# Attention with keys in the partitions of the scores, and one written-out order for TensorE

## The chip, the cores and the metric

The kernel runs on one core of a Trainium2 chip. The metric is the device time of one execution in microseconds (us). The core has five engines that run their own instruction streams: TensorE (PE; its weight loads are listed as PEld), VectorE (DVE), ScalarE (ACT), GpSimd (POOL) and SyncE (SP), which here issues all DMA transfers.

## The reference

One transformer block on 2048 tokens of width 1024, in float32: layernorm, causal attention with 16 heads of 64 and rotary embedding, layernorm, residual; then a gated feed-forward part with 4-bit weights (looked up from codes and scaled), again with layernorms and a residual.

```python
q = rotary((hidden @ Wq).reshape(b, s, 16, 64)); k = rotary(...Wk); v = ...Wv
logits = einsum('bhqd,bhkd->bhqk', q, k)
logits = where(causal, logits, -1e9) / sqrt(64)
attn = softmax(logits, axis=-1)
out = einsum('bhqk,bhkd->bhqd', attn, v).reshape(b, s, 1024) @ Wo
...
x = x + layernorm(attention(layernorm(x)))
x = x + layernorm(ffn(layernorm(x)))      # ffn: (silu(x Wg) * (x Wu)) Wd
```

## The kernel before

Float32 products are made of pieces. Each operand is split into a high part in the fp32r type (a ScalarE copy) and the rest (a VectorE subtraction); `split` does both. A product is then the sum of high x high, high x low and low x high, three passes on TensorE (`mm3`, lines 114 to 116).

The kernel has four stages. The ramp normalizes and transposes the input and makes q, k and v of the first two pairs of heads. The attention stage makes the q, k and v of the other six pairs (24 groups of `qkv`, one for each pair m and each 512 tokens c) beside the attention of the pairs that are ready. Then the output projection (`project`), the residual and the second transposition follow, and at last the feed-forward part, which the change does not touch.

Attention works on blocks: one head h and 512 queries (index J), 64 blocks in all. In a block the scores have the queries in the partitions: for each of its four 128-query tiles j and each 512 keys i, two products (lines 255 and 257: the high part of q against the stacked high and low parts of k, then the low part of q) and, on the diagonal, a third that adds the causal mask (line 259). Over a block's life:

- VectorE takes the row maximum of each 128x512 piece (line 261), ScalarE the exponential with that maximum as its bias, and sums it along the row at the same time (line 262).
- Small VectorE operations (lines 267 to 279) make one factor for each piece of a row, from the maxima and sums, with a reciprocal of two elements per partition; GpSimd multiplies the probabilities by it (line 284).
- For the product with v the keys must be in the partitions, so TensorE transposes each 128x128 piece of the probabilities (line 294, 2176 in all), `split` takes the two parts from the transposed bank, and two products with v (lines 298 and 299) add them up in the bank `o`. v holds its high part in columns 0 to 63 and its low part in 64 to 127, so the two halves of `o` are added at the end (lines 301 and 302).

There are eight PSUM banks: one for the q/k/v products and the projection ("F"), three for scores ("S"), three for transposes ("T"), one for `o` ("O").

The order of instructions on each engine is made by a scheduler, which lets the instruction streams run in a simulated time and takes what is ready, in the order of the program. Some q/k/v products are tied to a score product by a hand-made dependency (`after`, used in `pace`, with PACE = 0.85), so that they are spread over the attention beside them. All transfers go through SP's one queue. q, k and v pass through DRAM: `load_q` and `load_kv` bring a block's q and a head's k and v back in.

Of the kernel before, what the change touches and what calls it, by code (L numbers as in the profile page):

```python
# [22 lines left out]
D = 64  # L23
# [7 lines left out]
PACE = 0.85  # L31
# [3 lines left out]
BATCH = 2  # L35
STEP = 4
FIRST = (0, 1, 2, 3)
ORDER = (0, 3, 1, 2)
# [19 lines left out]
def block_kernel(ctx, tc, x, wq, wk, wv, wo, gu_codes, gu_scales, d_codes, d_scales, cos_sin, out):  # L58
# [12 lines left out]
    BANKS = {"F": 1, "S": 3, "T": 3, "O": 1}  # L71
    BANK_ORDER = ("F", "S", "S", "S", "T", "T", "T", "O")
# [8 lines left out]
    turn = [0]  # L81
# [5 lines left out]
    ident = const.tile([P, P], F32, name="ident")  # L87
    make_identity(nc, ident)
    ident_b = const.tile([P, P], BF, name="ident_b")
    V.tensor_copy(ident_b, ident)  # L90
    mask_f = slot("t2", [P, P], F32, "mask_f")
    G.memset(mask_f, 0.0)

    G.affine_select(out=mask_f, in_=mask_f, compare_op=ALU.is_ge, fill=MASK, base=0, pattern=[[-1, P]], channel_multiplier=1)
    mask_b = const.tile([P, P], BF, name="mask_b")
    V.tensor_copy(mask_b, mask_f)
# [6 lines left out]

    def f32(ap):
        return ap.bitcast(F32)
# [37 lines left out]
    def transposed(row, tiles, cs):  # L143

        for g in range(0, KE, 4):
            pt = bank("T", "pt").rearrange("p (k n) -> p k n", k=4)
            for k in range(4):
                T.transpose(pt[:, k], row[:, (g + k) * P : (g + k + 1) * P], ident)  # L148
            for k in range(0, 4, 2):
                d = tiles[(g + k) // 2]  # L150
                split(d[:, 0, :, cs], d[:, 1, :, cs], pt[:, k : k + 2])
# [54 lines left out]
    def qkv(m, c, ws, xs, ramp=False, pace=None):  # L206
# [3 lines left out]
        for n, w in enumerate(ws):  # L210
            o = bank("S" if ramp and n != 1 else "F", "qkv")
            for k in range(KE):
                mm = mm3(o, w[k], xs[k // 2][:, :, k % 2, :], k == 0, k == KE - 1)
                if k == 0 and pace:
                    pace(mm, n)
            t1 = slot("t2", [P, 512], F32, "t1")
            if n == 2:
                A.copy(t1, o)
                pv = bank("F", "pv").rearrange("p (t n) -> p t n", t=4)
                for t in range(4):  # L220
                    T.transpose(pv[:, t, :], t1[:, t * P : (t + 1) * P], ident)
# [5 lines left out]
            else:  # L227
                A.copy(t1, o)
                sh = slot("t2", [P, 512], F32, "sh")
                V.stream_shuffle(sh, t1, [i ^ 1 for i in range(32)])  # L230
                V.tensor_tensor(t1, t1, tab[:, 0, :], ALU.mult)
# [5 lines left out]


    def scores(J, q, k, anchors):

        prob = []
        nh = J + 1
        for j in range(4):
            t = 4 * J + j
            w = (t + 1) * P
            if j % BATCH == 0:
                mxs = small.tile([P, BATCH, 4], F32, tag="mxs", name="mxs")[:, :, :nh]
                sums = small.tile([P, BATCH, 4], F32, tag="sums", name="sums")[:, :, :nh]
            for i in range(nh):
                b, e = i * 512, min(i * 512 + 512, w)  # L250
                if j == 0:
                    prob.append(slot("pa", [P, 4, 512], F32, "prob"))
                diag = e == w
                s = bank("S", "s")[:, : e - b]
                mm = T.matmul(s, lhsT=q[:, 0, j * P : (j + 1) * P], rhs=k[:, b:e], start=True, stop=False)  # L255
                anchors.append(((anchors[-1][0] if anchors else 0) + e - b, mm))
                T.matmul(s, lhsT=q[:, 1, j * P : (j + 1) * P], rhs=k[:, b:e], start=False, stop=not diag)  # L257
                if diag:
                    T.matmul(s[:, e - b - P :], lhsT=ident_b, rhs=mask_b, start=False, stop=True)
                mx = mxs[:, j % BATCH, i : i + 1]  # L260
                V.tensor_reduce(mx, s, AX.X, ALU.max, negate=True)  # L261
                A.activation(prob[i][:, j, : e - b], s, AF.Exp, bias=mx, accum_out=sums[:, j % BATCH, i : i + 1])  # L262
            if j % BATCH < BATCH - 1:
                continue
            rc = small.tile([P, BATCH, 4], F32, tag="rc", name="rc")[:, :, :nh]
            if nh == 1:
                V.reciprocal(rc, sums)
            else:

                nm = small.tile([P, BATCH, 1], F32, tag="nm", name="nm")  # L270
                V.tensor_reduce(nm, mxs, AX.X, ALU.min)
                cf = small.tile([P, BATCH, 4], F32, tag="cf", name="cf")[:, :, :nh]
                V.tensor_tensor(cf, mxs, nm.to_broadcast([P, BATCH, nh]), ALU.subtract)
                A.activation(cf, cf, AF.Exp, scale=-1.0)
                sm = small.tile([P, BATCH, 1], F32, tag="sm", name="sm")
                V.tensor_tensor(sums, sums, cf, ALU.mult)
                V.tensor_reduce(sm, sums, AX.X, ALU.add)
                V.reciprocal(sm, sm)
                V.tensor_tensor(rc, cf, sm.to_broadcast([P, BATCH, nh]), ALU.mult)  # L279
            for i in range(nh):  # L280
                for jj in range(j - BATCH + 1, j + 1):
                    n = min(512, (4 * J + jj + 1) * P - i * 512)
                    p = prob[i][:, jj, :n]
                    G.tensor_scalar(p, p, rc[:, jj % BATCH, i : i + 1], 0.0, ALU.mult, ALU.add)  # L284
        return prob

    def weighted(h, J, prob, v):
        o = bank("O", "o")
        nk = 4 * J + 4
        for kb in range(nk):  # L290
            j0 = max(0, kb - 4 * J)
            pt = bank("T", "pt")
            for j in range(j0, 4):
                T.transpose(pt[:, j * P : (j + 1) * P], prob[kb // 4][:, j, kb % 4 * P : (kb % 4 + 1) * P], ident)  # L294
            cs = slice(j0 * P, 512)
            pw = slot("pw", [P, 2, 512], FR, "pw")
            split(pw[:, 0, cs], pw[:, 1, cs], pt[:, cs])
            T.matmul(o[:, cs], lhsT=v[:, kb, :], rhs=pw[:, 0, cs], start=kb == 0, stop=False)  # L298
            T.matmul(o[:, cs], lhsT=v[:, kb, :], rhs=pw[:, 1, cs], start=False, stop=kb == nk - 1)  # L299
        ol = slot("ol", [D, 512], F32, "ol")  # L300
        A.copy(ol, o[D:P, :])
        V.tensor_tensor(ol, o[:D, :], ol, ALU.add)
        load(at[J][h * D : (h + 1) * D, :], ol)

    def load_kv(h, k, v, cs):

        m, r = h // 2, h % 2 * D
        for a in range(2):
            load(f32(k[a * D : (a + 1) * D, cs]), ks[m][r : r + D, a, cs])
        load(f32(v[:, cs.start // P : cs.stop // P]), vs[m][cs, h % 2, :].rearrange("(t p) n -> p t n", p=P))  # L310

    def load_q(h, q, J):

        m, r = h // 2, h % 2 * D
        for a in range(2):
            load(f32(q[a * D : (a + 1) * D]), qs[m][r : r + D, :, J * 512 : J * 512 + 512])
# [13 lines left out]
    def both(*steps):  # L330
        for m, c in steps:
            qkv(m, c, first[m], xs[c], ramp=True)
# [8 lines left out]
    def new_kv():  # L341
        return slot("hd", [P, S], FR, "k"), slot("hd", [P, NT, P], FR, "v")

    def new_q():

        q = slot("hd", [P, 2, 2, 512], FR, "q")
        return [q[:, 0], q[:, 1]]

    def attend(h, J, q, k, v, anchors):
        weighted(h, J, scores(J, q, k, anchors), v)  # L350

    every = slice(0, S)
    parts = [slice(c * 512, (c + 1) * 512) for c in range(NC)]

    later = [(m, c) for m in range(2, KE) for c in range(NC)][:-2]
    ws = {}

    def group(m, c, xs=None, pace=None):
        if m not in ws:
            ws[m] = prep_qkv(m)  # L360
        qkv(m, c, ws[m], xs or load_x(c), pace=pace)

    for pair in range(KE - 1):
        anchors = []
        now = [later[g] for g in range(len(later)) if g * (KE - 1) // len(later) == pair]
        own = now and now[0][0] == pair
        for h in (2 * pair, 2 * pair + 1):
            k, v = new_kv()
            by_part = h == 0 or (own and h % 2 == 0)
            if not by_part:  # L370
                load_kv(h, k, v, every)
            if h % 2 == 0 and not own:
                if now[0][0] not in ws:
                    ws[now[0][0]] = prep_qkv(now[0][0])
                ready = load_x(now[0][1])
            order = FIRST if by_part else ORDER
            qj = {}
            for i, J in enumerate(order):
                if by_part:
                    if own and J == now[0][1]:  # L380
                        group(*now.pop(0))
                    load_kv(h, k, v, parts[J])
                if i % 2 == 0:
# [351 lines left out]
```

## Time and profile before

| what | value |
|---|---|
| time, median of 3 runs | 3121.71 us (3119.2 to 3123.59) |
| the profiled execution's own time | 3127.5 us |
| its span, first to last instruction | 3125.7 us |
| PE busy | 3003.9 us (96%) |
| DVE busy | 2161.1 us (69%) |
| ACT busy | 1831.5 us (59%) |
| POOL busy | 702.8 us (22%) |
| mean granted TensorE clock | 0.982 of full speed |

The durations in the next part come from the profiled execution, which is one execution; the span is what its engines' instructions cover, and its own time is a little longer. A group's row in the profile reads: line, engine, operation, output <- inputs by the program's names, shapes, number of instructions, then busy time in us and mean ns of one, and last the idle time of the engine just before these instructions and what ended most of it. The spans of matmuls overlap, because TensorE is pipelined: the distance from one start to the next is what a matmul costs, not its span.

### The profile page before, as it was taken

What the parts mean: (1) busy time and instruction counts of PE and PEld (TensorE: products, weight loads), DVE (VectorE), ACT (ScalarE), POOL (GpSimd) and SP (SyncE); (2) the same over time, 40 slices, a digit from 0 to 9 for tenths busy, and PEclk for the clock granted to TensorE, in tenths of its full rate; (3) what the DMA queues carried; (4) which work ended last, traced back from release to release, by engine and by line L of the source; (5) the groups of instructions that cost most, each with busy time, mean ns of one, the idle gap of its engine ahead of it and who ended that gap; (6) DMA issues with size and microseconds to landing.
All of it is one profiled execution on the core that took longest, in us unless ns stands there. A gap on an engine that the chain in (4) does not pass through costs nothing.

```text
span 3125.7 us, 43392 instructions
## 1 busy us (share of the span) xinstructions
PE 3003.9 (96%) x14656; PEld 2470.5 (79%) x14656; DVE 2161.1 (69%) x4428; ACT 1831.5 (59%) x3846; POOL 702.8 (22%) x888
## 2 busy tenths in 40 slices
PE   7979999999998999989988999999999999999998
PEld 6868888787877787778767888888888888888887
DVE  7457778687777777776574987666776669868322
ACT  3246667676766666676554876555665558657211
POOL 5344344343433443454222000000000000000000
PEclk9989999999999999999989999999999999999999
DMA  8777666557547656462355332222322226867785
GB/s 312 250 234 224 209 207 197 178 163 222 181 161 191 200 191 196 165 202 67 113 186 193 122 128 95 93 90 102 103 99 90 93 101 213 278 218 246 254 305 197
DMA packets 246495, 552.31 MB, mean 177 GB/s; under 512 B 20224, under 2 KB 110336, under 8 KB 219136
## 3 DMA queue, kind: packets, MB, share of 16 engines
q1 hardware_dynamic: 246272, 549.53, 53.8%
q8 instruction: 116, 1.90, 0.3%
q14 instruction: 107, 0.88, 0.1%
HBM read 403.70 MB, written 145.75 MB: 176 GB/s over the span
## 4 chain that ended last, share of the span: by engine, by line
PE 42%; DMA 3%; DVE 3%; ACT 1%; issue 1%; SPq 0%; DVEq 0%; POOLq 0%; POOL 0%; ACTq 0%
PE bk L114 13%; PE bk L116 13%; PE bk L115 13%; DMA cs<-in_d_codes 1%; DMA out<-xt 1%; PE pj L440 0%; PE pj L441 0%; PE pj L442 0%; DMA it<-ind 0%; DMA y<-yd 0%; DVE mp L511 0%; DMA cs<-in_d_scales 0%; PE pt L148 0%; DVE st L126 0%; DVE mp L504 0%
## 5 line engine op out<-in xcount | busy, mean ns | idle before, releaser
L498 ACT ACTIVATE ln<-cs,bias 128x512 f32<-128x512 f32 x910 | 611.8, 719 | 136.0 <-DVE mp L504 38.4
L114 PE MATMUL bk<-x,wt 128*128 128x512 f32 x1376 | 535.8, 390 | 0.0
L115 PE MATMUL bk<-x,wt 128*128 128x512 f32 x1376 | 535.4, 389 | 0.0
L116 PE MATMUL bk<-x,wt 128*128 128x512 f32 x1376 | 535.2, 389 | 0.0
L284 POOL TENSOR_SCALAR prob<-prob,rc 128x512 f32<-128x512 f32 (+3 forms) x640 | 408.1, 660 | 408.9 <-DVE rc L279 245.2
L262 ACT ACTIVATE prob<-s,mxs 128x512 f32<-128x512 f32 (+3 forms) x640 | 401.4, 630 | 161.2 <-DVE mxs L261 147.0
L121 DVE TENSOR_TENSOR pw<-pt,pw 128x512 fp32r<-128x512 f32 (+3 forms) x640 | 377.8, 602 | 135.1 <-ACT pw L120 133.4
L261 DVE TENSOR_REDUCE mxs<-s 128x1 f32<-128x512 f32 (+3 forms) x640 | 380.1, 602 | 96.3 <-PE s L257 57.7
L120 ACT CAST pw<-pt 128x512 fp32r<-128x512 f32 (+3 forms) x640 | 323.5, 526 | 165.4 <-PE pt L294 134.7
L132 POOL TENSOR_TENSOR rs<-ve,nhalf 128x1 f32<-128x1 f32 x64 | 40.0, 637 | 1552.2 <-DVE ve L130 1546.3
L294 PE MATMUL pt<-ident,prob 128*128 128x128 f32 x2176 | 347.1, 276 | 5.1 <-DVE pw L121 4.8
L294 PEld LDWEIGHTS pt<-ident,prob 128*128 128x128 f32 x2176 | 267.8, 142 | 59.3 <-issue 7.5
L255 PE MATMUL s<-k,q 128*128 128x512 f32 (+3 forms) x640 | 266.8, 417 | 36.9 <-ACT prob L262 35.4
L115 PEld LDWEIGHTS bk<-x,wt 128*128 128x128 f32 x1376 | 258.6, 188 | 53.9
L114 PEld LDWEIGHTS bk<-x,wt 128*128 128x128 f32 x1376 | 258.7, 188 | 53.5
L116 PEld LDWEIGHTS bk<-x,wt 128*128 128x128 f32 x1376 | 258.4, 188 | 53.7
L114 PE MATMUL bk<-wd,it 128*128 128x512 f32 x672 | 261.6, 389 | 1.2 <-DMA it<-ind 1.2
L115 PE MATMUL bk<-wd,it 128*128 128x512 f32 x672 | 261.4, 389 | 0.0
L116 PE MATMUL bk<-wd,it 128*128 128x512 f32 x672 | 261.3, 389 | 0.0
L299 PE MATMUL o<-pw,v 128*128 128x512 f32 (+3 forms) x640 | 250.6, 394 | 4.9 <-DVE pw L121 4.6
L298 PE MATMUL o<-pw,v 128*128 128x512 f32 (+3 forms) x640 | 247.1, 387 | 6.1 <-ACT pw L120 5.5
L114 PE MATMUL qkv<-xc,w 128*128 128x512 f32 x576 | 235.8, 409 | 13.0 <-ACT w L173 7.4
(124 smaller groups left out, 5514.2 us busy)
## 6 DMA issues: line engine op xcount, KB each, us to landing
xc<-xd SPq DMA_DIRECT2D x96, 1024.0 KB, 8.8
it<-ind SPq DMA_DIRECT2D x84, 1024.0 KB, 7.0
ind<-hl SPq DMA_DIRECT2D x84, 512.0 KB, 2.6
q<-qs SPq DMA_DIRECT2D x128, 256.0 KB, 7.1
cs<-in_gu_scales SPq DMA_DIRECT2D x172, 128.0 KB, 3.1
cs<-in_gu_codes SPq DMA_DIRECT2D x86, 256.0 KB, 2.9
tab<-in_cos_sin SPq DMA_DIRECT2D x32, 512.0 KB, 9.8
xd<-xr SPq DMA_DIRECT2D x16, 1024.0 KB, 6.8
```

What stands on the lines that cost most here:

```text
L114: r = T.matmul(o, lhsT=w[:, 0], rhs=xx[:, 0], start=first, stop=False)
L115: T.matmul(o, lhsT=w[:, 0], rhs=xx[:, 1], start=False, stop=False)
L116: T.matmul(o, lhsT=w[:, 1], rhs=xx[:, 0], start=False, stop=last)
L120: A.copy(hi, src)
L121: V.tensor_tensor(lo, src, f32(hi), ALU.subtract)
L255: mm = T.matmul(s, lhsT=q[:, 0, j * P : (j + 1) * P], rhs=k[:, b:e], start=True, stop=False)
L261: V.tensor_reduce(mx, s, AX.X, ALU.max, negate=True)
L262: A.activation(prob[i][:, j, : e - b], s, AF.Exp, bias=mx, accum_out=sums[:, j % BATCH, i : i + 1])
L284: G.tensor_scalar(p, p, rc[:, jj % BATCH, i : i + 1], 0.0, ALU.mult, ALU.add)
L294: T.transpose(pt[:, j * P : (j + 1) * P], prob[kb // 4][:, j, kb % 4 * P : (kb % 4 + 1) * P], ident)
L299: T.matmul(o[:, cs], lhsT=v[:, kb, :], rhs=pw[:, 1, cs], start=False, stop=kb == nk - 1)
L498: A.activation(ln, c8, AF.Identity, bias=bias_of[ab], scale=ab[0])
```

## The change

The scores are made with the keys in the partitions, so that the exponentials already lie as the product with v needs them. The 2176 transposes of line 294 are gone, and so are the small rescaling operations and GpSimd's scaling. What they did is done in other ways:

- Row maxima: `maxima` makes a separate score pass, queries in the partitions, from the high part of q alone with the stacked k, into the one bank "T"; VectorE reduces it as before. When a block's pieces are done, the minimum of the negated maxima is turned into one row by four small products with the identity and a ScalarE copy (`row`). That row is stored in partition 0 of a second q tile, against which a second k tile (`kb`) has ones, so that the maximum is subtracted inside the score product.
- Probabilities: `probabilities` makes two products per 128 keys (lines 375 and 376), the exponential is written into the same bank, and `split` takes both parts from there.
- Row sums: GpSimd adds the high parts of a block's probabilities (lines 393 and 395). The low parts are summed by TensorE: `vb` holds ones beside the high part of v, so that the second product with v (line 404) gives the sums in its upper 64 partitions, in a bank of its own ("L", two of them). At the block's end the GpSimd sums are split and added with two products against ones (`total`), and a VectorE reciprocal of 64x512 and a GpSimd product scale the output.
- TensorE's order: the work of the attention stage is laid out in steps, one for each 128 keys of a block. In each step come loads (rank 0), a score product (1), a maxima product (2), up to six products of the q/k/v groups or the projection (3, at 3.35 a step in the mean), and the products with v of two steps before (4). `chain` ties every TensorE instruction of this stage to the one before it.
- Banks: "T" has one in place of three, "L" two. Each block issues eight loads (three of k, three of q, two of v), and k and v are loaded block by block for every head.
- The masks and the identity are in fp32r in place of bf16, and the rotary product reads the bank in place of its copy in SBUF.

```diff
-    BANKS = {"F": 1, "S": 3, "T": 3, "O": 1}
+    BANKS = {"F": 1, "S": 3, "T": 1, "O": 1, "L": 2}
...
-                V.tensor_tensor(t1, t1, tab[:, 0, :], ALU.mult)
+                V.tensor_tensor(t1, o, tab[:, 0, :], ALU.mult)
...
+    def load_block(h, J):
...
+        for a in range(2):
+            load(f32(ka[a * D : (a + 1) * D, cs]), ks[m][r : r + D, a, cs])
+        load(f32(kb[D:, cs]), ks[m][r : r + D, 0, cs])
...
+        for a in range(2):
+            load(f32(q[a * D : (a + 1) * D, 0]), qs[m][r : r + D, 0, cs])
+        load(f32(q[D:, 1]), qs[m][r : r + D, 1, cs])
+        ts = slice(4 * J, 4 * J + 4)
+        load(f32(va[:, ts]), vs[m][cs, h % 2, :].rearrange("(t p) n -> p t n", p=P))
+        load(f32(vb[:, ts, :D]), vs[m][cs, h % 2, :D].rearrange("(t p) n -> p t n", p=P))
...
+    def chain(mm):
+        if tail:
+            after(mm, tail[-1])
+        tail[:] = [mm]
+        return mm
...
+    def maxima(h, J, j, i):
...
+        s = bank("T", "mx")[:, : e - b]
+        chain(T.matmul(s, lhsT=q[:, 0, j * P : (j + 1) * P], rhs=ka[:, b:e], start=True, stop=not diag))
+        if diag:
+            chain(T.matmul(s[:, e - b - P :], lhsT=ident_r, rhs=mask_q, start=False, stop=True))
...
+        V.tensor_reduce(mx[:, j, i : i + 1], s, AX.X, ALU.max, negate=True)
...
+            def row():
+                r = bank("T", "row")
+                for jj in range(4):
+                    chain(T.matmul(r[:1, jj * P : (jj + 1) * P], lhsT=nm[:, jj : jj + 1], rhs=ident_r, start=jj == 0, stop=jj == 3))
+                A.copy(q[:1, 1], r[:1])
...
+    def probabilities(u, h, J, kb):
...
+        chain(T.matmul(s[:, cs], lhsT=ka[:, ks_], rhs=q[:, 0, cs], start=True, stop=False))
+        chain(T.matmul(s[:, cs], lhsT=kb_[:, ks_], rhs=q[:, 1, cs], start=False, stop=diag is None))
+        if diag:
+            chain(T.matmul(s[:, diag], lhsT=ident_r, rhs=mask_k, start=False, stop=True))
...
+        A.activation(s[:, cs], s[:, cs], AF.Exp)
...
+        split(pw[:, 0, cs], pw[:, 1, cs], s[:, cs])
...
+        if kb == 0:
+            G.tensor_copy(acc, f32(pw[:, 0]))
+        else:
+            G.tensor_tensor(acc[:, cs], acc[:, cs], f32(pw[:, 0, cs]), ALU.add)
+
+    def weighted(u, h, J, kb):
...
+        chain(T.matmul(o[:, cs], lhsT=va[:, kb], rhs=pw[:, 0, cs], start=kb == 0, stop=end))
+        chain(T.matmul(ls[:, cs], lhsT=vb[:, kb], rhs=pw[:, 1, cs], start=kb == 0, stop=False))
+        if not end:
+            return
+        y = acc[:D, 1]
+        A.copy(y, o[D:, :])
+        V.tensor_tensor(y, o[:D, :], y, ALU.add)
+        a2 = slot("pb", [P, 2, 512], FR, "a2")
+        split(a2[:, 0], a2[:, 1], acc[:, 0])
+
+        def total():
+            chain(T.matmul(ls, lhsT=ones_l, rhs=a2[:, 0], start=False, stop=False))
+            chain(T.matmul(ls, lhsT=ones_l, rhs=a2[:, 1], start=False, stop=True))
+            V.tensor_tensor(y, ls[:D, :], y, ALU.add)
+            r = acc[:D, 0]
+            V.reciprocal(r, ls[D:, :])
+            G.tensor_tensor(y, y, r, ALU.mult)
+            load(at[J][h * D : (h + 1) * D, :], y)
...
+        later.append((4, total))
...
+    fill = rest()
+    for step in range(min(work), max(work) + 8):
...
+        for rank in range(5):
+            if rank == 3 and step >= 0:
+                for _ in range(MOST):
+                    if spent >= PACE * (step + 1):
+                        break
+                    mm = next(fill, GAP)
+                    if mm is GAP:
+                        break
+                    chain(mm)
+                    spent += 1
+            for e in work.get(step, ()):
+                if e[0] == rank:
+                    e[2](*e[3])
```

## The prediction

> **What bounds the kernel now.** I read the windows first, to find where the change can act. The ramp's last first-pass product starts at 173 us and the last product with v ends at 1545 us, so the attention stage is 1372 us of the 3125.7 us span; a window in the feed-forward part stands below it as a yardstick for TensorE at full rate.
>
> ```profile
> 173.00:1545.00 1372.00, 1303.77 (x7106) 1065.97 (x7104) 1005.13 (x2281) 899.16 (x2319) 577.57 (x758) 0.97 0.59 184
> 2000.00:3000.00 1000.00, 999.42 (x4410) 827.28 (x4409) 677.81 (x1176) 571.44 (x904) 0.91 (x2) 1.00 0.46 156
> ```
>
> After the window's length come PE, PEld, DVE, ACT and POOL busy time with counts, then clock, DMA share, GB/s. The lower row gives the price of one 512-wide product: 1000 us / 4410 = 0.227 us. The upper row shows TensorE nearly always occupied, VectorE 73%, ScalarE 66%, GpSimd 42%. The PE timeline then shows what a transpose costs:
>
> ```profile
> 600.62 0.23 PE L298 MATMUL o<-pw,v 128*128 128x128 f32 x1
> 600.69 0.61 PE L294 MATMUL pt<-ident,prob 128*128 128x128 f32 x4
> 601.05 0.30 PE L299 MATMUL o<-pw,v 128*128 128x128 f32 x1
> 601.20 0.62 PE L294 MATMUL pt<-ident,prob 128*128 128x128 f32 x4
> 601.58 0.48 PE L255 MATMUL s<-k,q 128*128 128x512 f32 x1
> ```
>
> From the start of four transposes to the next start are 0.36 and 0.38 us, 0.093 us each, not the 0.276 us of their modelled spans; a 128-wide product takes 0.07 to 0.15 us. Priced so, TensorE has in the stage: 1729 q/k/v products x 0.227 = 392; 100 small transposes 9; 2176 transposes x 0.093 = 202; the two score products 272 and the two products with v 272 (640 each; L257's 640 add up to 136 us from start to start); masks 14; 288 output-projection products 65. Together 1226 us, so 146 us are waits and slow clock. TensorE bounds the stage. The waits of PE are led by this row, a score bank that the exponential still reads:
>
> ```profile
> PE s L255 <- ACT prob L262: 35.4, 18, 14.4
> ```
>
> **The change on TensorE.** It removes 2176 transposes (-202 us) and the bf16 masks (-14). It adds a second hi-times-hi score pass for the maxima, 640 products in the shapes of L257 (+136), 512 masks in fp32r (0.07 to 0.15 us each; I take 0.11: +56, and 29 if they cost what the old ones did), 256 one-row products for the maxima (between 0.028, the shortest start-to-start after a transpose, and 0.093: I take +24, low end +7) and 128 products for the row sums (128 x 0.227 = +29). The scores and the products with v stay as many. Sum +29 us, with -15 as the low end. The transposes were cheap, so TensorE is not unloaded.
>
> **The change on VectorE.** These are the rows that it is costed from:
>
> ```profile
> L261 DVE TENSOR_REDUCE mxs<-s 128x1 f32<-128x512 f32 x448 | 303.4, 683 | 70.5 <-PE s L257 57.7 <-PE s L259 10.3
> L121 DVE TENSOR_TENSOR pw<-pt,pw 128x512 fp32r<-128x512 f32 x448 | 300.7, 683 | 112.3 <-ACT pw L120 111.1
> L231 DVE TENSOR_TENSOR t<-t,tab 128x512 f32<-128x512 f32 x50 | 52.2, 1043 | 18.9 <-DMA tab<-in_cos_sin 18.5
> L302 DVE TENSOR_TENSOR ol<-o,ol 64x512 f32<-64x512 f32 x63 | 42.7, 677 | 36.7 <-ACT ol L301 36.7
> L278 DVE RECIPROCAL sm<-sm 128x2 f32<-128x2 f32 x96 | 15.5, 161 | 1.8
> L271 DVE TENSOR_REDUCE nm<-mxs 128x2 f32<-128x6 f32 x32 | 4.8, 149 | 0.1
> ```
>
> Reduces and subtractions stay (640 of each). The small rescaling operations L267 to L279 go: -124 us by their rows. The rotary product reads the bank in place of SBUF; at 0.69 in place of 1.04 us, 48 x 0.35 = -17. Per block of one head and 512 queries (64 blocks) come a subtraction for the split of the sums (0.69), an addition like L302 (0.68), a minimum like L271 (0.15): +97. And one reciprocal of 64x512, where before it had two elements. Its price decides the case. Low bound: it streams like L302, 0.68 us. High bound: L261 at 512 and at 128 elements (683 and 282 ns) gives 1.04 ns an element; L271 without its six elements is then 143 ns, and 161 - 143 = 18 ns for the reciprocal's two elements, 9 ns each, 512 x 9 + 143 = 4.75 us. The row nearest in kind is the reciprocal itself, so I take the dear side, 4.5 us: 64 x 4.5 = 288 us (43 at the low end).
>
> [...]
>
> VectorE's total is 1005 - 124 - 17 + 97 + 288 = 1249 us, still under TensorE's 1226 + 29 + waits; so it is not the total but the place of the reciprocal that costs. Maxima have one bank (T, three before), and TensorE's order is chained: each step needs the reduce of the step before. A full step is 3.35 + 1 + 2 + 2 = 8.35 products x 0.227 = 1.9 us. Behind a 4.5 us reciprocal stand on VectorE the next reduce and the next subtraction, and behind the reduce the whole of TensorE, its paced fill too. The cover is what TensorE still has before its next maxima product: at most 1.9 us, at least 1.9 - 0.9 (reduce and its signal) = 1.0; I take 1.5. So 3.0 us x 64 = 192 us.
>
> **Other waits.** At each block's end the last reduce, the minimum, the one-row products and a ScalarE copy of 512 elements (nearest L301, 0.58 us) pass through that same bank, while TensorE has two score products (0.45 us) in between: copy 0.58 plus queue and signals, less 0.45, with some 0.3 before it, about 1.0 us x 64 = 64 (0 to 100). At six places the next weights are split, six operations of 0.70 us in a row on VectorE: 6 x 4 = 24. Of the 146 us before I keep half, 73 (loads, restarts at low clock). Some of these fall inside a reciprocal's wait: -60. Sum 192 + 64 + 24 + 73 - 60 = 293 against 146: +147.
>
> **ScalarE, GpSimd, queues.** ScalarE loses 640 accumulator reads of 202 ns (-129) and gains 64 row copies and 64 splits (+77); hidden. GpSimd exchanges 640 scalings for additions with two SBUF inputs:
>
> ```profile
> L284 POOL TENSOR_SCALAR prob<-prob,rc 128x512 f32<-128x512 f32 x448 | 318.0, 727 | 391.4 <-DVE rc L279 245.2 <-ACT prob L262 24.4 <-PE pt L294 23.7
> ```
>
> Its rotary addition L233 takes 1.30 us, so 384 full additions 499, narrow ones at 2.17 ns an element (L450 at 1024 elements against L233 at 512) 141, 64 copies 47 (at L284's 0.73), 64 closing products 83, with the rotary work 125 and weights and residuals 29: 924 us of about 1550, one addition of 1.3 us in a 1.9 us step and four buffers of probabilities. I cost it at nothing; the four buffers hide it. SP issues eight loads per block, 512 in place of 212; issues take 0.47 us (median), 300 x 0.47 = 141 us more on a queue that waits most of the time, and bytes rise from 64 to 74 MB at a DMA share of 0.59. Hidden, unless a late q or k holds the chained TensorE.
>
> [...]
>
> **Sum.** +29 +147 = +176 us. The profiled execution took 3127.5 us (span 3125.7), 5.8 above the median 3121.7; the forecast is put on the median: about 3300 us, own range 3200 to 3400.
>
> **Rivals.** (a) The reciprocal streams at 0.68 us, and the fixed order wins: VectorE falls to 1004 us, no 192 us wait; waits 64 + 24 + 73 - 40 = 121 in place of 146, or 60 if the row chain is covered; TensorE between -15 and +29. That is 3122 - 25 + 7 = 3104, down to 3020. For it: the score waits of ACT (35.4 us) and the transposes' bank go. Against: two elements already show 18 ns. It is faster as long as the reciprocal is under about 1.7 us (cover 1.5). Chance 0.19. (b) The reciprocal is cheap, but one bank for maxima, each reduce in a queue 73% full, stops TensorE by 0.15 us a step: 640 x 0.15 = 96, with 29 less 25: 3122 + 100 = 3222. Chance 0.10. (c) GpSimd becomes the bound: additions at 1.73 us (upper quartile of L232's 64) make 384 x 0.43 = 165 us more, 1090 in all, and with rotary work in bursts the four buffers run out; on top of the forecast some 100 us: 3400. Against: 42% busy before. Chance 0.08. Forecast 0.63.
>
> **Numbers.** A measurement of this kernel tells 0.2% (6 us) from no change. Faster: (a) nearly whole, 0.18; same 0.04; slower 0.78. The range 3100 to 3400 leaves out the faster half of (a) and the upper edge of (c).
>
> **What would show it.** A reciprocal row near 4.5 us x64; PE waits led by the maxima product on VectorE's reduce, around 3 us each; the stage ending near 1720 us; transposes gone while PE's start-to-start sum stays within 30 us. A reciprocal row under 1 us, or GpSimd over 80% busy, would make me wrong.

## The result, and the profile after

The changed kernel takes 3574.0 us (median of 4 runs, 3568.6 to 3580.3) against 3122.7 us for the kernel before in the same measurement: ratio 1.1445, 95% interval [1.142, 1.147], 451 us more. The forecast was slower, at 3300 us with a range up to 3400.

The first view is the windows over the attention stage, now from 181 us (end of the ramp's products) to 1997 us (last product with v): 1816 us in place of 1372, so 444 of the 451 us are lost in this stage. Columns as before: length, PE, PEld, DVE, ACT, POOL busy with counts, granted clock, DMA share, GB/s.

```profile
181.00:1997.00 1816.00, 1435.47 (x6171) 1131.49 (x6170) 1255.93 (x1934) 899.07 (x1723) 919.93 (x825) 0.89 0.46 143
```

VectorE has 251 us more work, ScalarE as much as before, GpSimd 342 us more; none of them is full. TensorE executes fewer products (6171 in place of 7106), and its granted clock fell from 0.97 to 0.89. The waits of PE in this stage tell for whom it stood still (us in total, times, longest):

```profile
PE mx L343 <- DVE mxs L349: 128.7, 82, 4.1
PE qkv L230 <- DVE t L248: 74.5, 35, 6.4
PE row L360 <- DVE nm L353: 74.4, 27, 5.9
PE qkv L230 <- ACT w L185: 25.4, 5, 9.9
PE qkv L230 <- issue: 19.4, 9, 4.8
PE mx L343 <- ACT q L361: 10.1, 28, 0.9
```

The leading wait before was one of 35.4 us. Three of the new ones name VectorE: its reduce in the maxima bank, its rotary product in the q/k/v bank, its minimum. PE's waits in the stage name transfers for 0.8 us only, so nothing shows that the eight loads of a block held it. The groups of VectorE and GpSimd in the stage:

```profile
L349 DVE TENSOR_REDUCE mxs<-mx 128x1 f32<-128x512 f32 x445 | 305.9, 687 | 245.6 <-PE mx L343 225.9 <-PE mx L345 17.0
L418 DVE RECIPROCAL acc<-l 64x512 f32<-64x512 f32 x63 | 211.6, 3359 | 0.9
L416 DVE TENSOR_TENSOR acc<-l,acc 64x512 f32<-64x512 f32 x63 | 42.7, 678 | 16.3 <-PE l L415 15.6
L248 DVE TENSOR_TENSOR t<-qkv,tab 128x512 f32<-128x512 f32 x49 | 33.3, 679 | 0.2
...
L395 POOL TENSOR_TENSOR acc<-acc,pw 128x512 f32<-128x512 f32 x384 | 494.7, 1288 | 476.4 <-ACT pw L132 471.6 <-DMA kb<-ks 1.8
```

The reciprocal takes 3.36 us. Note the first row's end: VectorE itself is idle for 226 us before its reduces because the maxima product has not come. TensorE waits for VectorE and VectorE for TensorE, so VectorE's idle third need not be spare time; b1 and k1 below test that.

One block's end in the timeline shows how they hold each other (start us, us, engine, what, and in brackets the idle time before):

```profile
1056.02 3.36 DVE L418 RECIPROCAL acc<-l 64x512 f32<-64x512 f32 x1
1056.05 0.40 PE L376 MATMUL s<-q,kb 128*128 128x512 f32 x1
...
1059.41 0.42 DVE L349 TENSOR_REDUCE mxs<-mx 128x1 f32<-128x256 f32 x1
...
1059.76 0.68 DVE L248 TENSOR_TENSOR t<-qkv,tab 128x512 f32<-128x512 f32 x1
...
1059.89 0.79 PE L343 MATMUL mx<-ka,q 128*128 128x512 f32 x1 [3.44 <-DVE mxs L349]
1060.35 1.28 DVE L133 TENSOR_TENSOR pw<-s,pw 128x512 fp32r<-128x512 f32 x2
1060.49 0.29 PEld L230 LDWEIGHTS qkv<-xc,w 128*128 128x128 f32 x1 [0.31 <-DVE t L248]
...
1061.09 0.63 PE L231 MATMUL qkv<-xc,w 128*128 128x512 f32 x1
```

When the reciprocal begins, TensorE has one score product left. Then its next instruction is a maxima product, whose bank waits for the reduce behind the reciprocal: 3.44 us of standstill. After it a q/k/v product waits for the rotary product in the same queue, and the next two starts lie 0.60 us apart, not 0.23: the waits continue in small, and TensorE resumes at a lower clock (the profile's granted clock is 0.50 from 1058.4 to 1065.1 us, and 1.00 after it).

This block has less cover than most. Read in the trace for all 64 reciprocals, a stop being a distance of over 0.48 us between the starts of two products, TensorE goes on for 1.15 us in the mean after the reciprocal's start (1.40 in the median). Then, in 63 of 64 blocks, it stops: 42 times before a maxima product and 14 times before a one-row product. A stop lasts 3.29 us in the mean, 207 us in all, and ends 1.08 us in the mean after the reciprocal's end (0.65 in the median).

Adding up distances from one matmul's start to the next in both stages splits the loss. Distances over 0.48 us, less one product each, are waits: 79 us before, 442 after. What distances of 0.32 to 0.48 us have over 0.227 is taken for low clock: 26 and 120 us (after the change 543 of these 719 begin while the granted clock is 0.5; before it 68 of 186). The rest is work: 1266 and 1254 us. So TensorE's work hardly changed (-12), waits are +363 us and slow clock +94. By the product before which TensorE stands, 157 us of the 442 are at maxima products, 132 at q/k/v products and 94 at one-row products.

### The profile page after: what moved, and what is told of

It is laid out like the page before. It is cut to its first block, busy times and chain, and to the rows that moved or that the text cites. A ratio compares the mean times of both kernels' runs of the same rounds, so it can differ in the third digit from the quotient of the medians.

```text
span 3570.8 us, 41916 instructions
## 1 busy us (share of the span) xinstructions
PE 3140.8 (88%) x13760; PEld 2540.7 (71%) x13760; DVE 2403.2 (67%) x4077; ACT 1822.7 (51%) x3238; POOL 1050.4 (29%) x964
## 4 chain that ended last, share of the span: by engine, by line
PE 70%; DVE 15%; DMA 4%; ACT 4%; issue 4%; POOL 2%; SPq 0%; POOLq 0%; DVEq 0%; ACTq 0%
PE bk L126 13%; PE bk L127 13%; PE bk L128 13%; DVE acc L418 4%; PE qkv L230 4%; PE mx L343 4%; PE qkv L231 4%; PE qkv L232 4%; PE l L404 3%; PE o L403 3%; PE s L375 3%; PE s L376 3%; DVE mxs L349 2%; DVE pw L133 2%; DVE acc L416 1%
## 5 line engine op out<-in xcount | busy, mean ns | idle before, releaser
L395 POOL TENSOR_TENSOR acc<-acc,pw 128x512 f32<-128x512 f32 (+3 forms) x576 | 639.9, 1111 | 679.0 <-ACT pw L132 671.6
L349 DVE TENSOR_REDUCE mxs<-mx 128x1 f32<-128x512 f32 (+3 forms) x640 | 388.8, 607 | 339.0 <-PE mx L343 225.9
L381 ACT ACTIVATE s<-s 128x512 f32<-128x512 f32 (+3 forms) x640 | 331.4, 519 | 540.1 <-PE s L376 313.5
L133 DVE TENSOR_TENSOR pw<-s,pw 128x512 fp32r<-128x512 f32 (+3 forms) x640 | 383.4, 605 | 85.2 <-ACT pw L132 78.9
L343 PE MATMUL mx<-ka,q 128*128 128x512 f32 (+3 forms) x640 | 283.5, 443 | 144.3 <-DVE mxs L349 130.4
L230 PE MATMUL qkv<-xc,w 128*128 128x512 f32 x576 | 257.5, 447 | 120.4 <-DVE t L248 74.5
L132 ACT CAST pw<-s 128x512 fp32r<-128x512 f32 (+3 forms) x640 | 333.8, 523 | 36.2 <-POOL acc L395 4.4
L343 PEld LDWEIGHTS mx<-ka,q 128*128 128x128 f32 x640 | 133.8, 209 | 223.5 <-DVE mxs L349 173.5
L403 PE MATMUL o<-pw,va 128*128 128x512 f32 (+3 forms) x640 | 250.0, 391 | 10.2 <-ACT pw L132 9.8
L375 PE MATMUL s<-q,ka 128*128 128x512 f32 (+3 forms) x640 | 256.6, 401 | 1.5 <-DVE pw L133 1.5
L404 PE MATMUL l<-pw,vb 128*128 128x512 f32 (+3 forms) x640 | 250.3, 391 | 8.2 <-DVE pw L133 8.2
```

Of the source, the lines that this page charges most:

```text
L133: V.tensor_tensor(lo, src, f32(hi), ALU.subtract)
L230: yield T.matmul(o, lhsT=w[k][:, 0], rhs=xx[:, 0], start=k == 0, stop=False)
L343: chain(T.matmul(s, lhsT=q[:, 0, j * P : (j + 1) * P], rhs=ka[:, b:e], start=True, stop=not diag))
L349: V.tensor_reduce(mx[:, j, i : i + 1], s, AX.X, ALU.max, negate=True)
L375: chain(T.matmul(s[:, cs], lhsT=ka[:, ks_], rhs=q[:, 0, cs], start=True, stop=False))
L395: G.tensor_tensor(acc[:, cs], acc[:, cs], f32(pw[:, 0, cs]), ALU.add)
```

## The experiments

Each run was measured beside the kernel before, which stood at 3123 to 3126 us. "Waits" and "slow" below are the parts just defined. Runs with a star leave out a part of the result (the division by the row sums, most of the row sums, or, in b1, the output itself in favour of its inverse) and serve the timing alone.

| run | edit | us | ratio to before [95%] | waits | slow |
|---|---|---|---|---|---|
| after | | 3574 | 1.1445 [1.142, 1.147] | 442 | 120 |
| e1_copy* | reciprocal to copy | 3359 | 1.0745 [1.0723, 1.0766] | 289 | 68 |
| e2_rot | rotary product from SBUF | 3511 | 1.1228 [1.1208, 1.1249] | 398 | 107 |
| e3_split | reciprocal in four pieces | 3491 | 1.1164 [1.114, 1.1187] | 390 | 100 |
| e4_t2 | two maxima banks | 3497 | 1.1185 [1.1159, 1.1212] | 408 | 103 |
| f1_copy_rot_t2* | e1 + e2 + e4 | 3260 | 1.0432 [1.0394, 1.0471] | 226 | 50 |
| g1_all* | f1 + weights early + row later | 3202 | 1.0242 [1.0217, 1.0268] | 183 | 47 |
| g3_no_t2* | g1 without e4 | 3262 | 1.0441 [1.0414, 1.0468] | 219 | 56 |
| e6_split_rot_t2 | e3 + e2 + e4 | 3394 | 1.0861 [1.0835, 1.0887] | 331 | 83 |
| g2_no_chain | after, no ties | 3608 | 1.1545 [1.1517, 1.1573] | 461 | 137 |
| h1_no_adds* | after, no GpSimd additions | 3568 | 1.1424 [1.1397, 1.1451] | 437 | 120 |
| b1_recip_before* | before + reciprocal | 3273 | 1.048 [1.0453, 1.0507] | 189 | 51 |
| b2_rot_before | before + rotary from the bank | 3135 | 1.0039 [1.0023, 1.0054] | 82 | 22 |
| k1_all_recip | g1, reciprocal whole | 3390 | 1.0853 [1.0833, 1.0872] | 322 | 88 |
| k2_all_split | g1, reciprocal in pieces | 3355 | 1.073 [1.0699, 1.0761] | 287 | 74 |
| k3_all_columns | g1, reciprocal of 128x4 | 3220 | 1.0307 [1.0285, 1.0329] | 157 | 39 |
| k4_all_no_chain* | g1, no ties | 3253 | 1.0415 [1.0393, 1.0437] | 188 | 73 |

**The reciprocal alone.**

```diff
-            V.reciprocal(r, ls[D:, :])
+            V.tensor_copy(r, ls[D:, :])
```

> The reciprocal of line 418 is replaced by a VectorE copy from the same bank to the same place, so the output is scaled by the sums and not by their inverse; all else stays. Changed kernel: 3574 us, reciprocal 3.36 us x64. Theory A (the long reciprocal holds the next reduce back, and with it TensorE): a copy of about 0.65 us takes 2.7 us x 64 = 173 us out of VectorE's queue at places where TensorE has about 1 us of cover, and the slow-clock time that these waits cause shrinks too, so 3574 - 110 to - 200, 3375 to 3465, and the maxima product's and the one-row product's waits (157 and 94 us now) fall by more than half. Rival B (one bank for maxima is too few whatever the reciprocal takes): under 50 us, above 3525. If A were all of the loss, the kernel would be back at 3123.

It gave 215 us, above the range of theory A, for 64 x (3.36 - 0.69) = 171 us less of VectorE. Waits fell by 153 us and slow clock by 52 (120 to 68): that is how more than the 171 us came off the time. PE's waits in this run:

```profile
PE qkv L230 <- DVE t L248: 66.6, 36, 3.7
PE row L360 <- DVE nm L353: 36.4, 28, 3.1
PE mx L343 <- DVE mxs L349: 35.9, 55, 1.4
PE qkv L230 <- ACT w L185: 33.6, 5, 9.2
```

The waits on the reduce and the minimum fell to a third and to a half; the one on the rotary product stayed (66.6 us; 74.5 in the changed kernel). The 233 us that remain over the kernel before are not the reciprocal's.

**The rotary product.**

```diff
-                V.tensor_tensor(t1, o, tab[:, 0, :], ALU.mult)
+                V.tensor_tensor(t1, t1, tab[:, 0, :], ALU.mult)
```

> The rotary product of line 248 reads the copy in SBUF again and not the bank, as in the kernel before. Theory C (the bank F, one for all q/k/v products, is freed only when this VectorE product has come through its queue; 132 us of waits before the next q/k/v product): the bank is freed by the ScalarE copy, so these waits fall to some 40 us as before and the time falls by 60 to 120 us, to 3455 to 3515. Rival: the wait only moves to the next late thing (maxima product on its reduce), 0 to 25 us, above 3550.

63 us, inside the range of theory C. In this run the wait on L248 is no longer among PE's largest, but part of what it was came back before the maxima product:

```profile
PE mx L343 <- DVE mxs L349: 152.7, 95, 4.1
PE row L360 <- DVE nm L353: 85.8, 32, 5.9
```

**Length or total.**

```diff
-            V.reciprocal(r, ls[D:, :])
-            G.tensor_tensor(y, y, r, ALU.mult)
+            A.copy(r, ls[D:, :])
+            def piece(k):
+                cs = slice(k * P, k * P + P)
+                V.reciprocal(r[:, cs], r[:, cs])
+                if k == 3:
+                    G.tensor_tensor(y, y, r, ALU.mult)
...
+            piece(0)
+            for k in range(1, 4):
+                later.append((k + 1, partial(piece, k)))
```

> ScalarE copies the sums out of the bank, and VectorE takes the reciprocal in four pieces of 64x128, one in each of four steps (about 0.9 to 1.0 us each). VectorE's total work stays (up to 30 us more), ScalarE gets 64 x 0.58 us more. Theory A' (what costs is that one operation is longer than TensorE's cover of some 1 to 1.5 us, not VectorE's total): nearly the whole gain of leaving the reciprocal out, at least 70% of it. Rival (VectorE's total is what binds): less than 30% of it, since the total is the same.

83 us, 39% of what leaving it out gave: between the two ranges, and nearer to the rival. Of PE's waits, the one before the maxima product stayed as it was (128.7 us in the changed kernel), and the one on the minimum fell from 74.4:

```profile
PE mx L343 <- DVE mxs L349: 128.3, 94, 4.0
PE row L360 <- DVE nm L353: 29.5, 28, 4.6
```

Length counts for something, the total for more; but the pieces also read SBUF in place of the bank and cost ScalarE a copy, so this run alone doesn't separate the two.

**A second bank for maxima.**

```diff
-    BANKS = {"F": 1, "S": 3, "T": 1, "O": 1, "L": 2}
+    BANKS = {"F": 1, "S": 2, "T": 2, "O": 1, "L": 2}
```

> Maxima get two banks and the scores two in place of three; the reciprocal stays. Theory B (the single bank ties each maxima product to the reduce before it): a second bank adds a step of cover (about 1.9 us), so that the waits before the maxima product (157 us) nearly go, 3574 - 100 to - 200. Rival (the scores need their third bank): the waits come back before the score products, and the time stays within 40 us of 3574 or rises.

77 us, below theory B and above its rival's. PE's waits show why both were half right: the maxima product waits 4.2 us in place of 130, and the scores, with a bank less, wait for the same queue instead. These two now lead:

```profile
PE qkv L230 <- DVE t L248: 100.2, 42, 6.4
PE s L375 <- DVE pw L133: 97.6, 57, 5.5
```

**Three together, and five.** The next edits ask for the weights of the next pair once each old one has been used (`prep_w` within the last group of the pair) and put the one-row products a step later:

```diff
-            later.append((1, row))
+            later.append((2, row))
...
-            ws = prep_qkv(m)
+            ws = ready or prep_qkv(m)
+            ready = []
+            def used(n):
+                if m < KE - 1:
+                    ready.append(prep_w((wq, wk, wv)[n], m + 1, (0.125, 1.0, 1.0)[n]))
```

> Three edits together: copy in place of the reciprocal (the division is left out), rotary product from SBUF, two banks for maxima and two for scores. Alone they gave -215, -63 and -77 us against 3574. If they are three separate waits, the sum: 3574 - 355 = 3219. If they are one and the same lateness of VectorE's queue that shows at three places, the later two find little left: 3290 to 3359.

> The three edits of the run before and two more: the split of the next weights is asked for as soon as each of the old ones has been used (waits of 34 us before q/k/v products on ScalarE's weight copies), and the one-row products come a step later (wait of 55 us on the minimum in the run without reciprocal). The division is left out. Theory (each of these is a wait of TensorE's fixed order for a late engine, and its work is no longer than before: 1247 us in the stage against 1266): back near the kernel before, 3100 to 3180. Rival (the fixed order itself loses, wherever the late engine is): stays above 3220.

Three together give 314 us of 355: 3260 lies between the two expectations (3219, and 3290 to 3359), so most of each is its own and 41 us are shared. The last two give 58 us more. At 3202 the kernel, still without the division, is between the two expectations again, 77 us above the one before, and its waits (183 us) are still twice those of the kernel before. Its leading one, with the score banks at two:

```profile
PE s L377 <- DVE pw L133: 60.4, 54, 4.7
PE qkv L230 <- issue: 31.0, 16, 3.2
PE row L362 <- DVE nm L355: 18.8, 11, 3.3
```

> As the run with all edits (3202 us), but with the banks of the changed kernel again: one for maxima, three for scores. If the second bank for maxima is worth 77 us also without the reciprocal and the other waits, 3260 to 3290. If its worth was that of cover behind the reciprocal, and the third score bank is worth as much, 3180 to 3220.

3262: the second maxima bank is worth 60 us also without the reciprocal, so it is not cover for that alone.

**The order of TensorE.** The ties are taken out (`chain` returns its product only), in the changed kernel and later in g1.

> The changed kernel without the ties between TensorE's instructions: the scheduler orders them by readiness in its own simulated time; all else stays, reciprocal and banks too. If the written-out order is what loses (a wait at one place stops all of TensorE), the time falls by over 100 us. If the order of the scheduler meets the same late reduces and banks, since an engine's stream is fixed before the run in either case, it stays within 60 us of 3574 or is longer.

> The run with 3202 us (division left out) without the ties between TensorE's instructions. If the written-out order is behind the 78 us that remain, 3120 to 3170. If it helps or makes no difference, as with the reciprocal in place (3608 against 3574), 3190 to 3260.

Without the ties both are slower, by 34 and 50 us. The ties are not what loses: without them the changed kernel meets the same late reduces (178.8 us before the maxima product in g2_no_chain). The program still lists the work step by step in these runs, so an order laid out in another way was not tested.

**All parts that leave nothing out.**

> Nothing is left out here: the reciprocal in four pieces out of SBUF, the rotary product from SBUF, two banks for maxima and two for scores. Alone they gave -83, -63 and -77 us. With two banks for maxima the cover of a step grows to some 3 us, more than a piece of 0.9 us needs: 3574 - 223 = 3351 if they add up, and 3300 if the pieces are now hidden. If VectorE's total in these steps binds (a step of 1.9 us against 1.5 + 0.9 us), above 3400.

3394: 180 of 223 us. That is between the expectations, 43 us above the plain sum and 6 below the 3400 from which VectorE's total was to bind. The pieces were not hidden by the second bank.

**GpSimd.**

```diff
-        else:
-            G.tensor_tensor(acc[:, cs], acc[:, cs], f32(pw[:, 0, cs]), ALU.add)
```

> The changed kernel without GpSimd's 576 additions of the probabilities (the row sums then lack all but the first 128 keys' high parts). GpSimd loses some 640 us of work. My theory: they are hidden behind the four buffers, 3574 -30 to +10. Rival (GpSimd bounds the steps, or its reads hold back VectorE's operations with two SBUF inputs): -100 us or more.

6 us. The additions are hidden, as the prediction had it, and neither rival holds. What the second names can be measured in the kernel before: its rotary product, with two SBUF inputs (L231), took 0.63 to 0.68 us the 3 times that GpSimd stood idle, and 1.08 in the mean the 52 times it ran beside GpSimd's product L232 alone. In the changed kernel the rotary product reads the bank and took 0.68 us beside GpSimd.

**The parts in the kernel before.** `b1` adds `V.reciprocal(ol, ol)` after line 302; `b2` lets line 231 read `o`.

> The kernel before with one operation more per block: a VectorE reciprocal of the block's 64x512 output in its place, so the attention output that is stored is its inverse; 64 x 3.36 = 215 us of VectorE. The score and transpose banks are three each here and VectorE is 73% busy in the stage (1005 of 1372 us), with 367 us idle. Theory A (the reciprocal costs so much in the changed kernel because one bank and one chained order give it no cover): here most is absorbed, 3125 + 20 to + 100. Rival (a 3.4 us operation on VectorE stops any such pipeline for its length): + 150 to + 215, 3275 to 3340.

> The kernel before with the rotary product reading the bank and not the copy in SBUF, that part of the change alone. Undoing it in the changed kernel gave 63 us. If it costs by holding the one bank of the q/k/v products for a VectorE queue, it costs here too, less in the measure in which VectorE's queue is shorter: +15 to +60 us. If it only hurts behind a reciprocal, 0 or a little gain (0.35 us x 48 = 17 us less on VectorE): -5 to +10.

The reciprocal costs 148 us here, 69% of its 213.5 us of work, though three score and three transpose banks stand by and 367 us of VectorE were idle: my theory A fails, and the rival's range is missed by 2 us only. So the cost needs neither the single maxima bank nor the chain of ties. The waits that lead in b1:

```profile
PE s L255 <- ACT prob L262: 69.6, 56, 13.9
PE o L299 <- DVE pw L121: 30.9, 32, 2.4
PE o L298 <- DVE ol L302: 21.3, 7, 7.5
```

The same in the kernel before:

```profile
PE s L255 <- ACT prob L262: 35.4, 18, 14.4
PE o L299 <- DVE pw L121: 4.6, 7, 1.3
PE o L298 <- DVE ol L302: 0.3, 1, 0.3
```

The rotary product costs 10 us here (ratio 1.0039), the upper end of the second expectation; in the changed kernel 63. The q/k/v products wait 2.6 us for it in b2 and 74.5 in the changed kernel. That the fuller VectorE queue makes the difference fits this, but no run changed the queue alone.

**What of the reciprocal costs, with all other edits in place.**

```diff
+            sums = acc[D : D + 1, 0]
+            A.copy(sums, ls[D : D + 1, :])
+            def columns():
+                c = bank("T", "col")
+                for jj in range(4):
+                    chain(T.transpose(c[:, jj : jj + 1], sums[:, jj * P : (jj + 1) * P], ident[D : D + 1, D : D + 1]))
...
+                V.reciprocal(rc, c[:, :4])
+                def rows():
+                    for jj in range(4):
+                        chain(T.transpose(ls[:D, jj * P : (jj + 1) * P], rc[:, jj : jj + 1].to_broadcast([P, D]), ident))
+                    V.tensor_tensor(y, ls[:D, :], y, ALU.mult)
```

> All edits of the run with 3202 us, but the whole reciprocal back in its place; nothing is left out. The cover of a maxima product is now two banks, some 3 us. If the cost is the length beyond the cover, it shrinks to well under half of 215 us: 3230 to 3300. If a 3.36 us operation stops the pipeline for its length whatever the banks (148 us in the kernel before): 3202 + 150 to + 215 = 3350 to 3417.

> The same with the reciprocal in four pieces in four steps; nothing is left out. If length is what costs, pieces of 0.9 us are under the cover and the time comes within 60 us of 3202. If VectorE's total in these steps costs (1.5 + 0.9 us against a step of 1.9 us, so some 2 us of lateness gather over four steps), half or more of what the whole reciprocal costs remains: 3280 to 3350.

> The same with the sums turned by four TensorE transposes into 128x4, one reciprocal of four elements (about 0.18 us), four transposes back and a VectorE product; nothing is left out. Adds 64 x 8 transposes of 0.1 us = 51 us to TensorE and takes the 0.69 us copy of the run with 3202 us off VectorE, a product of 0.68 us comes back. If VectorE's time is all that the reciprocal costs: 3202 + 30 to + 80. If each more hand-over between the engines in a fixed order costs a wait (three here): above 3300.

Whole, it costs 188 us against g1, inside the second range; in pieces 153, 81% of that and 5 us above the upper range; with four elements 18, less than the 30 to 80 expected. The stage's windows of g1 and of the three, in this order:

```profile
173.00:1634.00 1461.00, 1304.89 (x6169) 1055.49 (x6168) 1117.14 (x1931) 889.79 (x1722) 947.49 (x824) 0.95 0.58 178
```

```profile
173.00:1821.00 1648.00, 1366.11 (x6169) 1094.63 (x6168) 1266.69 (x1931) 891.72 (x1722) 938.12 (x824) 0.92 0.51 158
```

```profile
173.00:1773.00 1600.00, 1348.95 (x6171) 1080.15 (x6170) 1252.40 (x2120) 926.93 (x1785) 952.91 (x824) 0.93 0.53 162
```

```profile
174.00:1651.00 1477.00, 1344.71 (x6674) 1089.43 (x6673) 1097.50 (x1994) 928.28 (x1785) 868.89 (x761) 0.97 0.59 176
```

g1 and the whole reciprocal differ by that operation alone: VectorE's busy time rises by 150 us and the stage by 187. From the four elements to the whole it is 169 and 171 us, from the four elements to the pieces 155 and 123 (the profiled execution of the pieces was 16 us faster than their median); there TensorE, ScalarE and GpSimd differ a little too. VectorE is busy for 74 to 78% of each stage, and yet most of what is put on it shows. A second bank gives TensorE more to do behind the whole reciprocal, but not enough: it goes on for 1.96 us in the mean in place of 1.15, and then stops 60 times for 2.67 us, 45 times before a score product. The reciprocals of the run with four elements:

```profile
L427 DVE RECIPROCAL rc<-col 128x4 f32<-128x4 f32 x64 | 11.3, 177 | 23.7 <-PE col L425 23.6
```

This version leaves nothing out, is 354 us faster than the changed kernel and 97 us slower than the one before. No run beat the kernel before.

## Why the prediction was right and wrong

The direction and its chief cause were right: the reciprocal is the largest single item, it stops TensorE mostly before the maxima product, and GpSimd and TensorE's work decide nothing. The size was not: +176 us forecast, +451 measured. What failed is the sum of the waits, 293 against 146. By distances between starts, waits and slow clock went from 105 us to 562, +457 in place of +147. By the steps:

- *TensorE's work, +29 us, low end -15.* Measured -12. Right in substance, which fits transposes as cheap as their starts said.
- *The reciprocal's price, 4.5 us.* Measured 3.36. The pieces of 128 columns (0.90 us) give (3359 - 900) / 384 = 6.4 ns an element. The 9 ns came from 18 ns over two elements; at 6.4 ns they make 13, and where the other 5 come from no run shows. Streaming at the 1.04 ns of a reduce is excluded.
- *The cover, "I take 1.5. So 3.0 us x 64 = 192 us".* The cover was mis-sized, and the dear price hid it. It was meant as what TensorE has left, less a part of the reduce behind the reciprocal. TensorE goes on for 1.15 us in the mean, as I thought, but its stop ends 1.08 us after the reciprocal: next to nothing is left of the cover. That 192 is so near to the 207 us of these stops, and to the 215 that e1 gave back, is luck: with 3.36 us and a cover of 1.5 the sum is 64 x 1.86 = 119.
- *"It is not the total but the place of the reciprocal that costs".* This holds for the smaller part. A second bank left 188 us of it (k1), four pieces 61% (e3) and 81% (k2), and in the kernel before, with three banks and without the chain of ties, it costs 148.
- *The rotary product, "48 x 0.35 = -17".* This step failed by sign. I priced the operation on VectorE (0.68 us measured, as said) and put no wait into the sum for what it holds: the only bank of the q/k/v products, until VectorE's queue has come to it. It cost 63 us.
- *The single bank for maxima.* The sum lets it cost behind the reciprocal only; by itself it stands in rival (b), in place of the reciprocal and not beside it. A second bank is worth 77 us, and 60 without the reciprocal.
- *The one-row products, 64 us, and the weights, 24.* Waits of 94 and 25 us were measured, by starts and by the profile; the two edits together gave 58 in g1. About right in size.
- *Half of the waits before kept, and -60 for overlap.* The half was wrong: slow clock alone went from 26 to 120 us. In the changed kernel, of the 31 stops of over 3 us that begin at full clock, 22 end at half clock; of the 36 of 2.0 to 2.5 us, one. The overlap was of the right size: three edits together gave 41 us less than each alone.
- *The rivals.* (a), a streaming reciprocal, fell with the 3.36 us. (b) was half there, as a part of the loss and not in its place. (c) fell with the 6 us of h1.

The edits account for 372 of the 451 us (3574 to 3202), with the division left out; k3, which leaves nothing out, recovers 354. The 79 us that remain in g1 lie in waits for VectorE's subtraction, in 31 us that the profile puts down to no engine, and in others; what would remove them stays open. Why VectorE's total shows almost in full at 75% busy is argued, not shown alone: its own stream is in a fixed order too, and it stands idle 226 us for a maxima product that waits for the operation before.

## What to carry to other kernels

When an engine off the bottleneck is joined to it by few banks and fixed orders, its idle share may be no reserve: test it by putting work on it, as b1 did (148 us for 213.5 us of work on an engine 73% busy), before an operation is moved there. Ask of a moved read which bank it keeps, and in whose queue. An elementwise reciprocal of a row that stands in 64 partitions alike was dear here (188 us in k1); with the row turned, so that each partition has four elements, it cost 18.

## What was not expected of the hardware

A reciprocal on VectorE cost 6.4 ns an element (0.90 us for 128 columns in e3, 3.36 for 512 in the changed kernel), six times a reduce or a subtraction (1.04 ns, from 683 and 282 ns at 512 and 128 columns in the kernel before), and 0.18 us for four in k3. A transpose of one partition to a column, and of a broadcast column back, eight a block, added some 49 us of work to TensorE in k3 (1281 against 1232 in g1), 0.1 us each. And low clock is worth counting: where waits rose by 363 us, slow starts rose by 94, and each run of the changed kernel whose waits fell clearly has fewer of these, from 120 us to 107 in e2, 68 in e1, 47 in g1 and 39 in k3.
